# A two-layer cross-attention kernel: the order of three engines in layer 2 written out, five step places per slot, and image values masked in DRAM

## The chip, the core and the metric

The kernel runs on one core of a Trainium2 chip. TensorE (PE in the profile) multiplies matrices into PSUM; VectorE (DVE), ScalarE (ACT) and GpSimd (POOL) do the elementwise work; SyncE (SP) issues nearly all DMA transfers, and ScalarE issues a few. Each engine takes its instructions in the order in which they stand in its own stream, and waits on semaphores for what other engines and transfers deliver. The metric is the device time of one launch in microseconds, lower is better; a run is compared with runs of the kernel before on the same chip.

## The reference

Two cross-attention layers follow each other on 16 sequences of 256 tokens (width 320, 20 heads of 16). The context has 252 text tokens (77 in layer 1) and image tokens; the last 4 (layer 1: all behind the first 77) are the image tokens. Layer 2, cut to what matters:

```python
q = heads(hidden_states @ W_q)
probs_t = softmax(einsum(q, heads(text_ehs @ W_k)) * attn_scale)
text_out = einsum(probs_t, heads(text_ehs @ W_v))
attn_scores = einsum(q, heads(ip_ehs @ W_k_ip)) * attn_scale
qsem = _l2norm(einsum('bhst,bte->bhse', probs_t, text_ehs))
sem = einsum('bhse,bne->bhsn', qsem, _l2norm(ip_ehs))
probs_ip = softmax(attn_scores + SEM_SCALE * sem) * spatial_mask
out = (text_out + einsum(probs_ip, heads(ip_ehs @ W_v_ip))) @ W_out + b_out + residual
```

Layer 2 needs the norm of a probability-weighted context row for each head and token (`_l2norm` of `qsem`). The kernel gets it from the Gram matrix G of the context: the norm squared is p^T G p, with p the unnormalised probabilities.

## The kernel before

The work is cut into slots of four heads: five slots (groups) per sequence, so 80 slots in layer 1 (k = 0 to 79) and 80 in layer 2 (k = 80 to 159), with two more to drain. A slot of layer 2 (`slot1`, L866) emits, in this order:

- `both1(k, 0)` (L774): transposed scores of slot k into PSUM tile T (L788), plain scores of slot k + 2 into S (L793). VectorE takes the row maxima of S (L794) and copies the image scores out (L810); ScalarE takes the exponentials of T (L800). S has a single buffer (`scores`, L92), so the next scores wait for L794 and L810.
- `attend1(k-2)` (L855): the sum of probabilities times values (L861) and of the norms (L863) into PSUM tile P; then `settle1` (L896): VectorE transposes P (L906), divides (L909, L910).
- `both1(k, 1)`, the other half of the tokens.
- `norm1(k-1, u, n)` (L843), four calls: p^T G in PSUM (L848, four or three matmuls of 128x512), multiplied by p on VectorE (L851) and summed (L853: on GpSimd for u = 0, on VectorE for u = 1).
- `rounded1(k, u)` (L834): the high half of p on ScalarE (L838), the low half on GpSimd (L839).
- `stacks(k + 4)`: SP loads the stacked queries and keys of slot k + 4; `maxima(k + 2)`: the maxima of slot k + 2 turned (L826), copied by ScalarE (L828) and sent by two transfers that ScalarE itself issues (L830).

All else of layer 2 is done by tasks, which are Python generators cut into steps: `k1` the keys (L466), `t1` the values and G (L471), `o1` the queries (L524, L528, L529), `i1` the image softmax (L917), `c1` the closing of a sequence (L964: `finish`, L754, with the output projection L520 and the residual L767). Each step has a due time in slots relative to the sequence's first slot; `fill(now)` (L1021) runs the steps that are due. A slot before has three places for steps, at 0.33, 0.67 and 1.0.

A matrix operand is used as a high and a low half, so most PSUM results are copied by ScalarE (the high half) and then subtracted by VectorE (the low half): L148 for keys, L529 for queries, L489, L495, L499 for G, L750, L752 for the closing. The context is split by ScalarE and GpSimd (L147, L148 with the tile cta).

The image values come in `image_softmax`: four rows of `vipd` are broadcast into the tile vb (its tile is named rs in the profile, L957), VectorE multiplies them by a mask (L961), and `close1` multiplies the result by the image probabilities on TensorE (L968). vb has one buffer.

What sets the order: only TensorE's stream stands as the code emits it (L1136, `manual_schedule(engines=PINNED)`). The streams of the other engines, SP's too, are put in order by the framework's scheduler.

## Time and profile before

| | us |
|---|---|
| median of 3 runs | 1527.03 (1524.84 to 1532.59) |
| the profiled execution's own time | 1525.5 |
| its span, first to last instruction | 1523.4 |
| granted TensorE clock, mean | 0.987 |
| start of layer 2's slot 80, first L788 | 696.0 |
| start of slot 159, the last with scores | 1491.3 |

The rows of the profile name a line of the kernel, an engine, and the tiles as output<-input. In a view of windows each pair is the busy time and the number of instructions of an engine in that stretch. In the chain of waits, each row is a start, a length and a piece of work; it is followed back from the end, and jumps to whatever released a piece.

### The profile page before, as it was taken

What the parts mean: (1) busy time and instruction counts of PE and PEld (TensorE: products, weight loads), DVE (VectorE), ACT (ScalarE), POOL (GpSimd) and SP (SyncE); (2) the same over time, 40 slices, a digit from 0 to 9 for tenths busy, and PEclk for the clock granted to TensorE, in tenths of its full rate; (3) what the DMA queues carried; (4) which work ended last, traced back from release to release, by engine and by line L of the source; (5) the groups of instructions that cost most, each with busy time, mean ns of one, the idle gap of its engine ahead of it and who ended that gap; (6) DMA issues with size and microseconds to landing.
All of it is one profiled execution on the core that took longest, in us unless ns stands there. A gap on an engine that the chain in (4) does not pass through costs nothing.

```text
span 1523.4 us, 35306 instructions
## 1 busy us (share of the span) xinstructions
PE 1452.4 (95%) x12522; PEld 1196.4 (79%) x12522; DVE 1180.6 (77%) x2584; ACT 956.0 (63%) x2073; POOL 1142.2 (75%) x1161
## 2 busy tenths in 40 slices
PE   7799999999999999799999999999999999999997
PEld 6788888888888878577777877777777777777765
DVE  5467676767676777777888888888888888788896
ACT  5557676767676866656656556656665665556563
POOL 3259797979797967787778678767877787778785
PEclk9899999999999999899999999999999999999999
DMA  6666565656565665465424443443444343434311
GB/s 217 165 176 175 163 175 163 175 162 175 163 175 163 168 182 136 104 188 171 156 86 138 121 139 115 127 130 109 136 117 138 108 144 110 150 98 120 115 42 59
DMA packets 226971, 215.38 MB, mean 141 GB/s; under 512 B 49714, under 2 KB 210708, under 8 KB 226796
## 3 DMA queue, kind: packets, MB, share of 16 engines
q1 hardware_dynamic: 225056, 211.83, 48.4%
q8 instruction: 100, 1.64, 0.5%
q10 hardware_dynamic: 1740, 1.30, 0.3%
q14 instruction: 75, 0.61, 0.2%
HBM read 122.17 MB, written 89.49 MB: 139 GB/s over the span
## 4 chain that ended last, share of the span: by engine, by line
PE 72%; POOL 10%; DVE 6%; DMA 5%; issue 3%; ACT 3%; SPq 0%; ACTq 0%; POOLq 0%; DVEq 0%
PE X L212 21%; PE X L848 14%; PE X L520 10%; PE P L711 7%; POOL wt L839 6%; PE S L650 5%; PE T L673 4%; PE T L788 3%; DMA rs<-vipd 3%; PE P L861 2%; DVE mn L794 2%; PE S L793 2%; POOL wt L853 2%; PE P L863 1%; PE X L569 1%
## 5 line engine op out<-in xcount | busy, mean ns | idle before, releaser
L679 POOL TENSOR_TENSOR P<-P,rs 128x512 f32<-128x512 f32 x320 | 411.4, 1307 | 161.3 <-ACT P L676 161.1
L839 POOL TENSOR_TENSOR wt<-P,ctb 128x512 f32<-128x512 f32 x212 | 271.0, 1292 | 117.7 <-ACT ctb L838 117.7
L848 PE MATMUL X<-ctb,gm 128*128 128x512 f32 x1120 | 293.7, 402 | 0.0
L676 ACT ACTIVATE P<-T 128x512 f32<-128x512 f32 x320 | 174.8, 593 | 106.2 <-PE T L673 99.1
L848 PEld LDWEIGHTS X<-ctb,gm 128*128 128x128 f32 x1120 | 199.5, 188 | 46.4 <-issue 0.4
L794 DVE TENSOR_REDUCE mn<-S 128x4 fp32r<-128x1008 f32 x160 | 191.6, 1197 | 31.3 <-PE S L793 31.3
L851 DVE TENSOR_TENSOR wt<-X,wt 128x512 f32<-128x512 f32 x240 | 164.2, 685 | 31.1 <-PE X L848 30.1
L800 ACT ACTIVATE P<-T 128x512 f32<-128x512 f32 x212 | 114.8, 593 | 47.7 <-PE T L788 47.2
L838 ACT ACTIVATE ctb<-P 128x512 fp32r<-128x512 f32 x212 | 124.2, 625 | 32.0 <-PE X L848 30.5
L652 DVE TENSOR_REDUCE mn<-S 128x4 fp32r<-128x716 f32 x160 | 142.5, 891 | 0.0
L711 PE MATMUL P<-P,vr 128*32 128x256 f32 x1920 | 126.9, 395 | 5.3 <-DVE mx L575 2.8
L520 PE MATMUL X<-hq,wE 128*128 128x256 f32 x768 | 114.4, 292 | 4.7 <-ACT hq L509 3.5
L520 PE MATMUL X<-ho,wF 128*128 128x256 f32 x768 | 108.6, 284 | 4.8 <-DVE ho L752 4.0
L212 PE MATMUL X<-cta,wA 128*128 128x252 f32 (+1 forms) x720 | 105.4, 290 | 7.3 <-ACT wA L147 5.8
L520 PEld LDWEIGHTS X<-hq,wE 128*128 128x128 f32 x768 | 103.6, 194 | 9.1 <-ACT hq L509 4.0
L520 PEld LDWEIGHTS X<-ho,wF 128*128 128x128 f32 x768 | 102.0, 190 | 9.9 <-DVE ho L752 4.4
L839 POOL TENSOR_TENSOR wt<-qsl,ctb 128x512 f32<-128x512 f32 x54 | 69.2, 1293 | 51.9 <-ACT ctb L838 49.8
L853 POOL TENSOR_TENSOR wt<-wt 128x512 f32<-128x512 f32 x80 | 103.3, 1292 | 0.0
L212 PEld LDWEIGHTS X<-cta,wA 128*128 128x128 f32 x720 | 93.8, 194 | 11.9 <-ACT wA L147 6.1
L722 DVE STREAM_TRANSPOSE nt<-P 128x512 f32<-128x512 f32 x80 | 57.1, 713 | 51.9 <-PE P L711 51.9
L147 ACT CAST kst<-X 128x252 fp32r<-128x252 f32 (+3 forms) x94 | 35.1, 373 | 95.3 <-PE X L212 75.5
L711 PEld LDWEIGHTS P<-P,vr 128*32 128x32 f32 x1920 | 56.5, 112 | 46.6 <-issue 9.6
(217 smaller groups left out, 3383.2 us busy)
## 6 DMA issues: line engine op xcount, KB each, us to landing
qd<-q SPq DMA_DIRECT2D x96, 384.0 KB
kd<-kst SPq DMA_DIRECT2D x73, 256.0 KB
rawc<-in_cT_dram SPq DMA_DIRECT2D x60, 256.0 KB
ks<-kd SPq DMA_DIRECT2D x160, 96.0 KB
qs<-qd SPq DMA_DIRECT2D x160, 96.0 KB
qs<-qd SPq DMA_DIRECT2D x60, 192.0 KB
ks<-kd SPq DMA_DIRECT2D x60, 192.0 KB
kd<-kst SPq DMA_DIRECT2D x21, 512.0 KB
```

The lines of the kernel that those rows point to most:

```text
L212: last = mm(out, lhs(a, k), rhs(b, k), start=i == 0, stop=i == len(terms) - 1)
L520: mm(pp, w(s, k, slice(m * 128, (m + 1) * 128)), a[:, t], start=i == 0, stop=i == len(terms) - 1)
L652: anchor(nc.vector.tensor_reduce(mn[:, t, 1], sp[:, :, T0:], axis=AX.X, op=ALU.max))
L676: exp = anchor(nc.scalar.activation(pt, st[p], AF.Exp, scale=SCALE))
L679: anchor(nc.gpsimd.tensor_mul(pt, pt, rs[:, t : t + 1].to_broadcast([128, 2, S])))
L711: mm(pv[32 * s : 32 * s + 32, o : o + S], v[:, vt, h : h + 32], P[k, s // 2][:, t, s % 2], start=vt < 2, stop=vt != 1,)
L794: anchor(nc.vector.tensor_reduce(maxes[k + 2][:, t], sp[:, :, :T1], axis=AX.X, op=ALU.max))
L838: nc.scalar.activation(R[k, u][:, t], P[k, u][:, t], AF.Copy, scale=0.5)
L839: anchor(nc.gpsimd.tensor_sub(W[k, u][:, t], P[k, u][:, t], f(R[k, u][:, t])))
L848: mm(yp, gm[:, gb], R[k, u][:, kt], start=i == 0, stop=i == len(blocks[n]) - 1)
L851: nc.vector.tensor_mul(product, yp, w[:, n])
L853: (nc.vector if u else nc.gpsimd).tensor_add(w[:, 0], w[:, 0], product)
```

## The change

Instructions on the engines are the same but for one: VectorE's multiplication by the mask (16 times) is gone. TensorE has the same 10555 matmuls, in another order. Five things change.

1. In slots 80 to 159 ScalarE, VectorE and GpSimd also keep the order in which the code emits them. SP's stream is still ordered by the scheduler. Slots 0 to 79 and the end are as before.
2. The slot has five places (0.2, 0.4, 0.6, 0.8, 1.0). `attend1` and `settle1` are parted: the sums go to TensorE where they were, the transposes and divisions come behind the 0.2 place. `stacks` and `maxima` stand at the end, in the order maxima, stacks.
3. The tasks' due times are new (a table, STEPS), on multiples of 0.2.
4. `late`: VectorE's low halves, sums of residuals and other late pieces go onto a list while `hold` is in force, from just before `rounded1(k, 1)` to `release` behind the next slot's `both1(k+1, 0)` and `attend1`; so they stand behind a row maximum. `settled()` empties the list at once wherever a following step needs them. `after_next` puts a low half behind the next unit of work.
5. The masked image values are made once in DRAM: task `w8` zeroes `spread_d` [16, 128, 384] and copies `vipd` into its places; `image_softmax` loads vb from there, some steps earlier. The mask tile is gone. The transposed sums hT have two buffers, and the last sequence's residual another tile.

```diff
+    def late(*makes):
+        if held[0]:
+            lates.extend(makes)
+        else:
+            for make in makes:
+                make()
...
+    def release():
+        held[0] = False
+        settled()
+    def settled():
+        while lates:
+            lates.pop(0)()
+    def after_next(make):
+        soon.append([2, make])
...
+    def weights8():
+        zero = buf("kb", [128, 3, 2, 96], FR, bufs=2, name="zero").rearrange("p a b c -> p (a b c)")
+        nc.gpsimd.memset(f(zero), 0.0)
+        yield
+        for b in range(0, B, 4):
+            dma(spread_d[b : b + 4].rearrange("b p c -> p b c"), zero[:, :CP].unsqueeze(1).to_broadcast([128, 4, CP]))
+            yield
+        for i in range(3):
+            for half in range(2):
+                row = 4 * min(2 * i + half, NG - 1)
+                for s in range(4):
+                    lo = 128 * i + 32 * s + 16 * half
+                    src = vipd.rearrange("(b n) c -> b n c", n=NIP)[:, :, lo : lo + 16]
+                    dma(spread_d[:, 32 * s + row : 32 * s + row + NIP, lo : lo + 16], src)
+                yield
...
         def evac(m, pp):
             nc.scalar.copy(qh[:, 0, m], pp)
-            nc.vector.tensor_sub(qh[:, 1, m], pp, f(qh[:, 0, m]))
+            late(lambda: nc.vector.tensor_sub(qh[:, 1, m], pp, f(qh[:, 0, m])))
 
         yield from project(l, wq[l], a, evac)
         qd = dram.tile([3, CP, S], F32, tag=f"qd{l}", name=f"qd{l}", bufs=2)
+        settled()
...
         for s in range(4):
             mm(pv[32 * s : 32 * s + 32, :S], zone, W[k, s % 2][:, 0, s // 2], start=False, stop=True)
-        settle1(b, g, pv)
+        return b, g, pv
...
+        summed = []
         if k > NS + 1:
-            yield lambda: attend1(k - 2)
+            yield lambda: summed.append(attend1(k - 2))
+        yield release
         yield lambda: both1(k, 1)
         if last:
             yield lambda: norm1(last, 0, 0)
-        yield 0.33
+        yield 0.2
+        for parts in summed:
+            yield lambda: settle1(*parts)
         if last:
             yield lambda: norm1(last, 0, 1)
         if mine:
             yield lambda: rounded1(k, 0)
-        yield lambda: stacks(k + LEAD)
+        yield 0.4
         if last:
             yield lambda: norm1(last, 1, 0)
+        yield 0.6
+        if last:
             yield lambda: norm1(last, 1, 1)
         if mine:
+            yield hold
+        if mine:
             yield lambda: rounded1(k, 1)
-        yield 0.67
+        yield 0.8
         yield lambda: maxima(k + 2)
+        yield lambda: stacks(k + LEAD)
         yield 1.0
...
+        vb = w1["vb"]
+        if hi == NG:
+            while b and ("taken", B + b - 1) not in results:
+                step(("c1", b - 1))
+            dma(vb, spread_d[b])
...
-        vb = w1["vb"]
-        dma(vb, vipd[NIP * b : NIP * (b + 1)].unsqueeze(0).to_broadcast([32, NIP, CP]))
         yield
         pT = w1["pT"]
-        nc.vector.transpose(pT, pi.rearrange("p f c -> p (f c)"))
-        nc.vector.tensor_mul(vb, vb, w1["bmask"])
+        late(lambda: nc.vector.transpose(pT, pi.rearrange("p f c -> p (f c)")))
...
+    STEPS = {
+        "k1": (-7, -6.2, -5.8, -5, -4.6, -3,),
+        "t1": (-3.2, -2.2, -2.2, -1.4, -0.4,),
+        "o1": (-6.8, -6.8, -6, -5.8, -4, -4,),
+        "i1": (6.8, 7.6, 7.6, 8.8, 9.2, 9.6, 10.6, 10.8, 10.8, 12.2,),
+        "c1": (12.8, 12.8, 13.4, 14, 14.2, 15.8,),
...
+    with tc.manual_schedule(engines=PINNED):
+        run(range(NS))
+    with tc.manual_schedule(engines=PINNED | {getattr(mybir.EngineType, e) for e in ("Activation", "DVE", "Pool")}):
+        run(range(NS, 2 * NS))
+    with tc.manual_schedule(engines=PINNED):
+        run(range(2 * NS, 2 * NS + 2))
         fill(999)
```

In a middle sequence of the changed kernel the five slots hold, beside the scores, attention and norms: (0) keys and two projections; (1) keys and values; (2) two image products, values, one half of G; (3) one image product, the other half of G, two projections; (4) two projections and keys. Before, they held: (0) projection, keys, projection; (1) values, projection, values; (2) both halves of G; (3) two projections, image product; (4) image product, keys, image product, projection, keys.

More of the change, by code (lines that the diff above doesn't have):

```diff
@@ L114, in buf, with hold, unit @@
         return t
+    held, lates, soon = [False], [], []
+    def late(*makes):
[4 more added lines that the diff above has]
+                make()
+    def hold():
+        held[0] = True
+    def release():
[6 more added lines that the diff above has]
+        soon.append([2, make])
+    def unit():
+        for x in soon[:]:
+            x[0] -= 1
+            if not x[0]:
+                soon.remove(x)
+                x[1]()
     def const_tile(shape, tag, dtype=F32):
@@ L465, in keys1 @@
             prod(kp, lambda s, k: w1["k"](s, k, ms), lambda s, k: ct(s, k)[:, :T1], 4)
-            halves(kst[:, 0, 0, :T1], kst[:, 1, 0, :T1], kp)
             nc.gpsimd.tensor_copy(kst[:, :, 0, T1:], f(kip[:, :, m, 4 * b : 4 * b + 4]))
-            keys_out(kd[1][b], m, kst)
+            nc.scalar.copy(kst[:, 0, 0, :T1], kp)
+            late(
+                lambda kst=kst, kp=kp: nc.vector.tensor_sub(kst[:, 1, 0, :T1], kp, f(kst[:, 0, 0, :T1])),
+                lambda kst=kst, m=m: keys_out(kd[1][b], m, kst),
+            )
             yield
@@ L510, in split @@
         order(eng.tensor_sub(hl[:, 3:5], src[:, 0:2], f(hl[:, 0:2])))
-        order(nc.vector.scalar_tensor_tensor(hl[:, 2], f(hl[:, 2]), neg, src[:, 2], op0=ALU.mult, op1=ALU.add))
+        third = lambda: order(
+            nc.vector.scalar_tensor_tensor(hl[:, 2], f(hl[:, 2]), neg, src[:, 2], op0=ALU.mult, op1=ALU.add)
+        )
+        if clock[0] >= NS:
+            after_next(third)
+        else:
+            third()
         return hl
@@ L632, in stacks1 @@
         qd = get("o1", b)
+        settled()
         for u in range(2):
@@ L947, in image_softmax @@
         z4 = small(1, "z4")
-        nc.vector.tensor_reduce(z4, a, axis=AX.X, op=ALU.add)
-        nc.vector.reciprocal(z4, z4)
+        late(
+            lambda: nc.vector.tensor_reduce(z4, a, axis=AX.X, op=ALU.add),
+            lambda: nc.vector.reciprocal(z4, z4),
+        )
         yield
+        settled()
         pool.tensor_mul(z4, z4, mk.unsqueeze(1).to_broadcast([128, n, 8]))
@@ L969, in rows @@
             nc.vector.tensor_add(hp, hT[:, p], hp)
-        y = yield from finish(1, b, load(x1d[b], "xc"), rows)
-        dma(out_d[b].rearrange("(k p) t -> p k t", p=128), y)
+        y = yield from finish(1, b, load(x1d[b], "xc" if b < B - 1 else "xq"), rows)
+        late(lambda: dma(out_d[b].rearrange("(k p) t -> p k t", p=128), y))
     def close0(b):
@@ L1135, in xattn2, with run @@
         begin()
-    with tc.manual_schedule(engines=PINNED):
-        for k in range(2 * NS + 2):
+    def run(slots):
+        for k in slots:
             clock[0] = k
```

114 lines of the change are left out of this document (70 added, 44 removed), and 16 rows, old and new, of the table STEPS.

## The prediction

> **What bounds the kernel now.** I read the page first, then windows by stage, windows over the five slots of one middle sequence, and the chain of waits through it.
>
> ```profile
> span 1523.4 us, 35306 instructions
> ...
> PE 1452.4 (95%) x12522; PEld 1196.4 (79%) x12522; DVE 1180.6 (77%) x2584; ACT 956.0 (63%) x2073; POOL 1142.2 (75%) x1161
> ```
>
> TensorE is busy 95% of the span, but a waiting matmul counts as busy, so that share is no floor. By stage (start:end length, then the busy time and count of PE, PEld, DVE, ACT, POOL, the clock, the DMA share, GB/s):
>
> ```profile
> 580.00:696.00 116.00, 101.90 (x946) 82.28 (x938) 89.07 (x192) 70.72 (x148) 92.61 (x86) 0.96 0.55 151
> ...
> 845.00:1362.60 517.60, 506.17 (x4181) 402.37 (x4180) 432.98 (x900) 308.39 (x670) 391.99 (x431) 1.00 0.42 126
> ...
> 1491.30:1523.40 32.10, 22.69 (x169) 16.03 (x168) 21.31 (x53) 9.03 (x22) 16.58 (x26) 0.99 0.18 60
> ```
>
> Layer 2's steady part is ten sequences in 517.6 us, 51.76 each. The clock is full there (1.00), so nothing is to be had from it. One sequence, slot by slot:
>
> ```profile
> 1000.30:1010.70 10.40, 9.94 (x85) 7.94 (x84) 8.66 (x17) 5.07 (x11) 5.27 (x7) 1.00 0.24 79
> 1010.70:1021.70 11.00, 11.00 (x92) 8.92 (x90) 8.45 (x17) 6.20 (x14) 8.93 (x12) 1.00 0.71 216
> 1021.70:1030.90 9.20, 9.20 (x83) 7.41 (x82) 8.23 (x19) 6.19 (x13) 6.48 (x10) 1.00 0.28 61
> 1030.90:1040.30 9.40, 9.15 (x77) 6.96 (x76) 7.54 (x18) 6.59 (x15) 8.60 (x10) 1.00 0.47 134
> 1040.30:1052.10 11.80, 11.37 (x93) 9.00 (x92) 10.56 (x23) 6.83 (x16) 9.94 (x10) 1.00 0.43 127
> sum 51.80, PE 50.67 PEld 40.23 DVE 43.44 ACT 30.87 POOL 39.20; mean PE 10.13 PEld 8.04 DVE 8.69 ACT 6.17 POOL 7.84
> ```
>
> And the chain of waits through it (start, length, work):
>
> ```profile
> 1000.57 0.04 DVE rs L961
> 1000.61 1.05 issue
> 1001.66 0.41 DVE kst L148
> 1002.06 1.11 DVE mn L794
> ...
> 1003.40 0.50 PE S L793 x4
> 1003.91 1.13 PE X L848 x4
> 1005.04 0.95 PE X L520 x8
> 1005.99 1.39 PE X L212 x12
> 1007.38 2.32 PE X L848 x10
> ...
> 1010.66 0.12 PE X L826 x2
> 1010.78 0.43 PE T L788 x4
> 1011.21 0.24 PE S L793 x4
> 1011.45 1.00 PE P L861 x16
> ...
> 1014.79 1.75 PE X L212 x12
> ...
> 1023.41 0.43 PE P L863 x8
> ...
> 1025.65 1.44 PE X L212 x12
> ...
> 1042.32 2.49 POOL wt L839 x2
> 1044.81 1.26 POOL cta L148
> ...
> 1049.26 0.45 PE X L968 x2
> ```
>
> These rows give TensorE's pieces without waits. Every slot has T and S twice, sums, norms and maxima: 2 x (0.43 + 0.24) + 1.00 + 0.43 + 1.13 + 2.32 + 0.12 = 6.34 us. A projection is 0.95, keys 1.39, values 1.75, half of G 1.44; an image product 0.25 (from its 0.45, less about 0.2 of drain that the next piece overlaps, an estimate). By slot: 6.34 + 0.95 + 1.39 + 0.95 = 9.6 against 10.4; 6.34 + 1.75 + 0.95 + 1.75 = 10.8 against 11.0; 6.34 + 2 x 1.44 = 9.2 against 9.2; 6.34 + 1.9 + 0.25 = 8.5 against 9.4; 6.34 + 0.5 + 2 x 1.39 + 0.95 = 10.6 against 11.8. The third slot comes out exactly, so the method holds. Floor 48.7 us, **loss 3.0 us per sequence**, in the first and the last two slots. VectorE, 43.4 of 51.8, is the next engine, GpSimd 39.2.
>
> **The change part by part.** *The mask multiplication.* In the chain it stands at a place where TensorE waits: VectorE waited for vb to land, multiplied, and only then came to the maximum on which the single S buffer hangs. Its row, its wait, and beside them the one other large VectorE operation with both inputs in SBUF, the third piece of hq:
>
> ```profile
> L961 DVE TENSOR_TENSOR rs<-rs,nt x16: 557/932/1200, 704.9 to 1509.1; 128x384 f32<-128x384 f32 x16
> ...
>   DMA rs<-vipd: 11.8, 15
> ```
>
> ```profile
> L511 DVE SCALAR_TENSOR_TENSOR hq<-hq,tmask,xq x32: 428/477/1504, 19.1 to 1389.0; 128x256 fp32r<-128x256 f32 x32
> ```
>
> Removing it frees 0.93 us of VectorE per sequence and 11.8 / 15 = 0.8 us of standing still. The first slot's loss (0.8) should go with it. VectorE's load falls to 42.5 per sequence.
>
> The spread of L961, 557 to 1200 ns, is that of an operation held up by a neighbour. The Trainium skill, SBUF — State Buffer, section "SBUF: two separate sides", says that a VectorE operation with two SBUF inputs and a GpSimd operation that reads SBUF lock each other out for a whole instruction; the trace agrees, with 1200 and 1504 ns at the top against 557 and 428 at the bottom.
>
> *The written order.* The loss of the last two slots (0.9 + 1.2) is one of order: in the chain GpSimd does two L839 pieces (2.49) and only then the second context split (1.26), on which the keys wait. In the new streams both splits stand early in the slot whose end holds the keys, ahead of GpSimd's norm sum; L853 for u = 0 stands ahead of the L839 pieces. Both have several us in hand, so the 2.1 us are recoverable. The five slots also become even: 6.34 + 1.39 + 1.9 = 9.6; + 1.39 + 1.75 = 9.5; + 0.5 + 1.75 + 1.44 = 10.0; + 0.25 + 1.44 + 1.9 = 9.9; + 1.9 + 1.39 = 9.6: still 48.7, and 42.5 / 48.7 = 87% for VectorE, so that small waits remain.
>
> *What it adds on the path.* A written order can't step around a wait. I followed VectorE's new stream against TensorE's pieces and find three such places.
> (a) At the end of slot (0), the low half of q is flushed by `settled()` ahead of the next maximum. It waits for ScalarE's copy, which stands behind the maxima's copy and two transfers that ScalarE issues:
>
> ```profile
> L830 ACTq DMA_DIRECT2D qs<-mt x160: 632/632/866, 689.3 to 1485.1; - x160
> ```
>
> The maxima's product ends about 8.7 into the slot. Copy about 0.4, two issues 1.3, q's copy 0.4: VectorE's piece starts at 11.0 and ends at 11.4, where the maximum could start at 9.65 + 0.8 = 10.45. That is 1.0 late. Second scores follow the first by T to T, 0.43 + 0.24 + 1.00 + 0.43 = 2.1, and need the maximum (1.11 plus a copy of about 0.15), so some 0.45 is in hand: 0.5 lost.
> (b) At the end of slot (2) the next T takes a PSUM bank that the closing's low half frees: about 10.0 after norms, two image sums, ScalarE's copies; 0 to 0.4, I take 0.3.
> (c) In slot (3) the last projection takes G's bank behind three low pieces: 0.3 to 0.4, I take 0.35.
> Transfers: `stacks` now goes out some 0.6 of a slot later, and SP's stream is short of slack. The trace of before has no wait of TensorE for a stack in the steady part, so this price isn't shown: bounded by 0 and by one landing, 2.9 (row below), per sequence. I take 0.15, near the lower end: a whole slot still lies between issue and use. Sum 1.3, so 3.0 - 1.3 = **1.7 us won per sequence**, and the 14 sequences between the first and the last give 24. The first shares its slots with the end of layer 1, the last lacks keys and values; half of it each, 2.
>
> *Masks in DRAM.* The zeroes are 16 x 128 x 384 x 4 B = 3.1 MB; at the 151 GB/s of the window from 580 on that is 21 us of DMA traffic where the share is 0.55, plus 24 small scatters. It falls into the last slots of layer 1, where queries and keys also pass through DRAM. Bounds: 0, if it fits between, and 14.1 (116.00 - 101.90, TensorE's idle time of that stage, doubled); I take 1, as SP's scheduler puts the pieces between the stacks.
>
> *The end.* The chain of waits at the end:
>
> ```profile
> 1506.17 2.90 DMA rs<-vipd
> ...
> 1509.09 0.04 DVE rs L961
> 1509.13 0.44 issue
> ```
>
> vb's last load is 3.4 us of the chain there. It now starts before the exponential and division of the image softmax, which then set the pace; I take 2 of 3.4 (bounds 0 and 3.4).
>
> *Sum:* 24 + 2 + 2 - 1 = 27. The profiled execution took 1525.5, 2.1 more than its span; 1498.5. The median of the runs shown is 1527.0, 1.5 above it: **1500 us**.
>
> **The rivals.**
> *All of the loss goes:* (a) to (c) are hidden because a bank or the order is better than I followed it. 14 x 3.0 = 42, with 2 x 1.5 and the end 3.4: 48 less, 1479. For it: the slots are even to 0.5 us. Against: VectorE at 87% with fixed places. 0.12.
> *One wait for another:* VectorE's order holds nearly as much as the scheduler's did, with S late in two slots of five; (a), (b), (c) at twice my price, 2.3, plus 0.3 of transfers leave 0.4 per sequence: 14 x 0.4 + 2 = 8 less, 1519. For it: three places found by hand are seldom all. 0.14.
> *GpSimd and VectorE lock each other out* at hq's third piece, L511's 1504 against 477, 1.0 us per sequence, as its new place stands beside GpSimd's: 1.7 - 1.0, 14 x 0.7 + 3 = 13 less, 1514. Against: in the new stream GpSimd has only a small copy there. 0.05. This is the rule of the SBUF page named above.
> *Stacks or maxima land late (slower):* ScalarE's L830 now stands in a fixed place, ahead of the exponentials, and some of them wait for an SP transfer that is issued in the same slot. If SP is held by the queries' round trip through DRAM, ScalarE and then TensorE wait one landing, 2.9 us, in each sequence: 1.7 - 2.9 = -1.2, 16 times, is 19 more; the end gives 2 back and the zeroes take 1: 1545. It decides from about 2 us of delay on SP. For it: keys come nearly half a slot later and their stack is wanted a slot and a half later. Against: no row with TensorE waiting on a stack before. 0.17.
> *The change doesn't do what it says* (the scheduler's order was the same in effect): 1527. The streams differ on all engines, so only 0.02.
>
> **How the numbers follow.** Main forecast 0.50, its own range 1488 to 1512; the rivals as given. 0.5% is 7.6 us, about what a measurement of this kernel can tell from no change. Faster (below 1519.4): 0.50 + 0.12 + 0.05 + half of the 0.14 = 0.74, and some of the late-landing case, which can come out mild: 0.77. Same: the other half, 0.02, and little of the rest, 0.08. Slower 0.15. The range leaves out the worst of full recovery and most of the late-landing case: 1476 to 1530.
>
> **What would show it.** A middle sequence of 50.0 us, with slots of 9.5 to 10.2; no wait of VectorE for rs; TensorE's wait for S (now L793) gone from slot (0), but 0.5 in slot (1); no wait of TensorE for the context split; VectorE about 42.5 per sequence. Wrong if TensorE waits for ks or qs, if ScalarE stands at its transfers, if the stage from 580 to 696 grows by over 3 us, or if a sequence still takes 51.5.

## The result, and the profile after

| | us |
|---|---|
| changed kernel, median of 6 runs | 1515.72 (1513.96 to 1520.13) |
| kernel before on the same chip, median of 6 runs | 1526.36 (1522.9 to 1532.59) |
| ratio, 95% interval | 0.9934 [0.9909, 0.9958] |
| profiled execution of the changed kernel, its span | 1518.7, 1516.9 |

The change is worth 0.66%, about 10 us where 27 were forecast: faster, and inside the widest predicted range (1476 to 1530), but 15.7 us above the forecast of 1500 us and outside the main forecast's own range of 1488 to 1512. The two profiled executions are 6.8 us apart, their spans 6.5.

The page of the changed kernel, its span and the load of its engines (lines of this kernel's code are about 70 to 90 higher than before: the exponentials' T is L864, S L869, the row maximum L870, the norms' matmul L926, the maxima's transfers L907):

```profile
span 1516.9 us, 35343 instructions
...
PE 1452.9 (96%) x12522; PEld 1204.3 (79%) x12522; DVE 1178.5 (78%) x2568; ACT 951.8 (63%) x2073; POOL 1145.8 (76%) x1162
```

Every engine is as busy as before to 0.7%: what the change won or lost is waiting, not work.

The windows by stage (same columns as before): the end of layer 1; the first ten slots of layer 2; ten steady sequences (slots 95 to 144).

```profile
580.00:690.70 110.70, 98.47 (x905) 81.04 (x903) 83.48 (x183) 68.61 (x145) 89.80 (x83) 0.92 0.57 152
690.70:796.90 106.20, 97.76 (x771) 76.93 (x772) 80.03 (x158) 60.69 (x131) 73.98 (x75) 0.95 0.39 118
847.40:1353.20 505.80, 501.14 (x4184) 403.88 (x4184) 433.02 (x891) 305.76 (x670) 394.00 (x431) 1.00 0.44 129
```

Beside them the same ten slots, 80 to 89, in the kernel before:

```profile
696.00:793.30 97.30, 92.76 (x772) 73.26 (x770) 81.27 (x166) 61.80 (x135) 75.85 (x80) 1.00 0.44 134
```

The steady part went from 517.6 to 505.8 us, 1.2 per sequence. The first ten slots, with 767 matmuls for 768, went from 97.3 to 106.2, and the granted clock fell to 0.95 there. Taken from the first T matmul of each slot in both traces:

| stretch | before | after | difference | forecast |
|---|---|---|---|---|
| to slot 80 | 696.0 | 690.5 | -5.5 | +1 |
| slots 80 to 89 | 97.3 | 106.2 | +8.9 | -2.7 |
| slots 90 to 149, 12 sequences | 621.2 | 607.5 | -13.7 | -20.4 |
| slots 150 to 154 | 46.3 | 48.9 | +2.6 | -1.7 |
| slot 155 to the end | 62.6 | 63.8 | +1.2 | -3 |

So this is a gain in the middle that is given back in part at both ends.

The stretches don't hold quite the same work, since the new due times put some of TensorE's pieces on the other side of a boundary. Counted by their starts in the two traces, the stretch to slot 80 has 17 matmuls of the keys fewer, slots 80 to 89 have five of them more and slots 150 to 154 twelve more; three image products fewer stand in slots 80 to 89, one projection fewer in slots 90 to 149, and these stand behind slot 155. With the lengths of the pieces (1.39 for twelve matmuls of the keys, 0.43, 0.95), the differences on equal work are, as an estimate, -3.5, +9.6, -12.8, +1.2 and -1.0. The ten steady sequences hold the same 4180 matmuls in both.

The five slots of a middle sequence, as windows:

```profile
897.90:907.60 9.70, 9.70 (x88) 7.91 (x88) 8.43 (x18) 5.72 (x12) 9.00 (x10) 1.00 0.13 43
907.60:917.70 10.10, 9.70 (x84) 7.73 (x84) 8.65 (x19) 5.40 (x11) 7.39 (x11) 1.00 0.83 263
917.70:928.00 10.30, 10.30 (x85) 8.38 (x83) 8.91 (x18) 6.33 (x16) 7.72 (x10) 1.00 0.56 159
928.00:938.70 10.70, 10.70 (x90) 8.56 (x91) 9.14 (x21) 7.09 (x18) 7.38 (x7) 1.00 0.44 116
938.70:948.40 9.70, 9.70 (x88) 7.83 (x86) 8.17 (x17) 6.01 (x13) 8.02 (x10) 1.00 0.20 58
sum 50.50, PE 50.10 PEld 40.41 DVE 43.30 ACT 30.55 POOL 39.50; mean PE 10.02 PEld 8.08 DVE 8.66 ACT 6.11 POOL 7.90
```

Slots (0) and (4) stand at 9.7, almost at their sum of 9.6; (1), (2) and (3) are 0.3 to 0.8 above theirs. The chain of waits through the same sequence says why:

```profile
905.31 0.95 PE X L587 x8
...
906.42 0.37 ACT mt L904
...
906.81 0.63 ACTq L907
...
907.48 0.63 ACTq L907
...
908.15 0.38 ACT q L595
...
908.56 0.42 DVE q L596
908.98 1.11 DVE mn L870
...
910.32 0.50 PE S L869 x4
...
923.71 0.86 PE X L1059 x4
...
927.85 0.78 PE T L864 x4
...
936.36 2.12 PE X L587 x16
```

The first eight rows are place (a) of the prediction, link by link: maxima's copy, two issues on ScalarE, q's copy, q's low half, the maximum, S. The last three rows price what the sum had estimated: two image products are 0.86 together, 0.43 each and not 0.25; the T at the start of slot (3) is 0.78 where a free one is 0.43 (place (b)); two projections in slot (3) are 2.12 instead of 1.91 (place (c)).

The start, slots 80 and 81: windows of the changed kernel, and the chain through the first of them.

```profile
698.70:704.00 5.30, 1.75 (x16) 1.17 (x14) 2.49 (x7) 3.72 (x9) 4.30 (x6) 0.88 0.49 161
704.00:710.50 6.50, 6.50 (x23) 5.08 (x21) 4.24 (x8) 2.29 (x5) 1.93 (x2) 0.58 0.60 197
```

```profile
700.41 0.64 ACTq L907
...
701.09 0.38 ACT ho L827
...
701.50 0.42 DVE ho L818
701.92 0.33 DVE q L596
...
703.61 0.80 PE S L869 x4
704.41 5.79 PE X L926 x14
```

TensorE has 1.75 us of work in 5.3 us, waiting for S behind the same kind of row: ScalarE's issues, the copy of the first layer's closing (ho), its low half, q's low half, the maximum. Then its granted clock is 0.58, and 14 norm matmuls take 5.79 us. Slot 81 is 16.0 us; before it was 11.0.

### The profile page after: what moved, and what is told of

It is laid out like the page before. It is cut to its first block, busy times and chain, and to the rows that moved or that the text cites. A ratio compares the mean times of both kernels' runs of the same rounds, so it can differ in the third digit from the quotient of the medians.

```text
span 1516.9 us, 35343 instructions
## 1 busy us (share of the span) xinstructions
PE 1452.9 (96%) x12522; PEld 1204.3 (79%) x12522; DVE 1178.5 (78%) x2568; ACT 951.8 (63%) x2073; POOL 1145.8 (76%) x1162
## 4 chain that ended last, share of the span: by engine, by line
PE 82%; DVE 6%; DMA 4%; ACT 2%; issue 2%; ACTq 1%; POOL 1%; SPq 1%; DVEq 0%; POOLq 0%
PE X L245 22%; PE X L926 17%; PE X L587 11%; PE P L780 6%; PE S L719 5%; PE T L742 4%; PE P L939 4%; PE T L864 4%; PE S L869 2%; PE P L941 2%; DVE mn L870 2%; ACTq L907 1%; PE X L637 1%; PE X L1059 1%; DMA kd<-kst 1%
## 5 line engine op out<-in xcount | busy, mean ns | idle before, releaser
L926 PE MATMUL X<-ctb,gm 128*128 128x512 f32 x1120 | 296.3, 407 | 0.7 <-ACT P L876 0.4
L870 DVE TENSOR_REDUCE mn<-S 128x4 fp32r<-128x1008 f32 x160 | 192.8, 1205 | 68.6 <-PE S L869 66.5
L926 PEld LDWEIGHTS X<-ctb,gm 128*128 128x128 f32 x1120 | 202.7, 190 | 51.2 <-ACT P L876 0.9
L929 DVE TENSOR_TENSOR wt<-X,wt 128x512 f32<-128x512 f32 x240 | 159.4, 682 | 5.5 <-PE X L926 5.5
L780 PE MATMUL P<-P,vr 128*32 128x256 f32 x1920 | 123.8, 388 | 3.6 <-DVE mx L643 2.6
L587 PEld LDWEIGHTS X<-hq,wE 128*128 128x128 f32 x768 | 101.2, 195 | 10.6 <-ACT hq L570 3.8
L245 PE MATMUL X<-cta,wA 128*128 128x252 f32 (+1 forms) x720 | 99.7, 285 | 5.5 <-ACT wA L180 5.5
L720 DVE TENSOR_REDUCE mn<-S 128x4 fp32r<-128x308 f32 x160 | 74.6, 466 | 22.8 <-PE S L719 22.7
L719 PE MATMUL S<-ks,qs 125*128 125x256 f32 x480 | 87.8, 306 | 1.2 <-DVE mn L721 1.2
```

The costliest lines, as they stand in the source:

```text
L245: last = mm(out, lhs(a, k), rhs(b, k), start=i == 0, stop=i == len(terms) - 1)
L587: mm(pp, w(s, k, slice(m * 128, (m + 1) * 128)), a[:, t], start=i == 0, stop=i == len(terms) - 1)
L719: mm(sp[:, h], Q[: XROW + T0, h, t * 128 : (t + 1) * 128], K[: XROW + T0, h], start=True, stop=True)
L780: mm(pv[32 * s : 32 * s + 32, o : o + S], v[:, vt, h : h + 32], P[k, s // 2][:, t, s % 2], start=vt < 2, stop=vt != 1,)
L870: anchor(nc.vector.tensor_reduce(maxes[k + 2][:, t], sp[:, :, :T1], axis=AX.X, op=ALU.max))
L926: mm(yp, gm[:, gb], R[k, u][:, kt], start=i == 0, stop=i == len(blocks[n]) - 1)
```

## The experiments

All kernels, with the ratio to the kernel before on the same chip, and lengths in us from the first T matmul of the slots in each profiled execution:

| kernel | median | ratio, 95% interval | slots 80-89 | slots 95-144 | slots 150-154 |
|---|---|---|---|---|---|
| before | 1526.36 | 1 | 97.3 | 517.6 | 46.3 |
| changed | 1515.72 | 0.9934 [0.9909, 0.9958] | 106.2 | 505.8 | 48.9 |
| e1 masks alone | 1517.99 | 0.9954 [0.9935, 0.9973] | 99.2 | 513.8 | 46.0 |
| e2 scheduler's order | 1519.83 | 0.9965 [0.9944, 0.9985] | 99.9 | 515.7 | 46.4 |
| e3 written from 90 | 1513.51 | 0.9927 [0.9900, 0.9954] | 95.9 | 506.7 | 48.1 |
| e4 written 90 to 149 | 1511.07 | 0.9911 [0.9884, 0.9938] | 97.6 | 505.5 | 50.6 |
| e5 q behind | 1508.80 | 0.9904 [0.9867, 0.9942] | 103.3 | 501.0 | 48.2 |
| e6 ho one unit later | 1518.43 | 0.9953 [0.9934, 0.9971] | 106.2 | 505.5 | 48.7 |
| e8 nothing held | 1545.79 | 1.0128 [1.0098, 1.0158] | 109.6 | 523.6 | 49.0 |
| e9 e5 + ho late | 1509.81 | 0.9887 [0.9853, 0.9920] | 105.7 | 501.2 | 47.4 |
| e10 mask back | 1527.94 | 1.0017 [0.9995, 1.0038] | 106.6 | 509.2 | 48.6 |
| e11 e5 + maxima by SyncE | 1527.64 | 1.0009 [0.9987, 1.0030] | 99.5 | 525.7 | 49.7 |
| e12 e5 + weights early | 1507.62 | 0.9873 [0.9838, 0.9908] | 105.4 | 501.5 | 47.5 |
| e13 e5 + SyncE at the start | 1504.82 | 0.9860 [0.9828, 0.9892] | 99.8 | 499.7 | 48.6 |
| e14 e5 + si after | 1503.07 | 0.9846 [0.9818, 0.9873] | 103.3 | 498.1 | 47.5 |
| e15 e13 + e14 | 1499.80 | 0.9823 [0.9795, 0.9852] | 100.5 | 497.7 | 47.5 |

The stretches of before and e1 differ from those of the others by the pieces named above. In e3 and e4, 21 matmuls of slot 89 stand behind the first T of slot 90, and slot 80 has five fewer, so their slots 80 to 89 hold 741 matmuls where the changed kernel's hold 767; in e4, 24 of slot 149 stand behind the first T of slot 150.

### Parting the change: masks, order, where the order begins

e1 is the kernel before with part 5 alone (the masked image values in DRAM and the task that makes them).

> The kernel before with part 5 alone: the image values masked once in DRAM, no multiplication on VectorE; places and orders as before. My sum gave the multiplication and its wait 0.8 us per sequence (slot (0) from 10.4 to about 9.6) and 2 at the end, less 1 for the zeroes: 12 less than before, about 1514, so as much as the whole change gave. The rival: VectorE's next piece takes the place of the wait, slot (0) stays over 10.1, and the time is 1522 to 1527.

The multiplication is gone, and the middle sequence falls from 51.8 to 51.4, all of it in slot (0) (10.4 to 10.0). That is half of the 0.8 that the prediction gave to it: the maximum is late for a second reason as well. In e1's trace the low half of the keys stands ahead of it and waits 1.38 us for ScalarE's copy, which stands behind the two issues of the maxima's transfers, the row of place (a).

e2 is the changed kernel with TensorE's stream alone fixed, so that the scheduler orders ScalarE, VectorE and GpSimd in layer 2:

```diff
-    with tc.manual_schedule(engines=PINNED | {getattr(mybir.EngineType, e) for e in ("Activation", "DVE", "Pool")}):
+    with tc.manual_schedule(engines=PINNED):
         run(range(NS, 2 * NS))
```

> The changed kernel with the scheduler's order on ScalarE, VectorE and GpSimd in layer 2 too; places, late pieces and masks as changed. If the written order is worth something as a whole, this is slower than the changed kernel's 1516, up to 1530. If it wins about 1.1 us per middle sequence and gives it back at both ends, the two are within 4 us, slots 80 to 86 are some 8 us shorter than in the changed kernel, and the middle sequences 0.5 to 1 us longer than 50.5.

The written order is worth 9.9 us in the ten sequences (515.7 against 505.8). Slot (3) wins 1.6 per sequence: 10.5 to 11.2 us written, 11.9 to 13.2 by the scheduler. In slot (1) the scheduler is better by 0.7, 9.46 against 10.13 and more, and at the start by 6.3 us. Slot (2) is 10.33 in both, and in all later kernels: no order decides it.

e3 and e4 begin the written order at slot 90, and e4 ends it at slot 149.

```diff
-        run(range(NS))
+        run(range(NS + 10))
...
-        run(range(NS, 2 * NS))
+        run(range(NS + 10, 2 * NS))
```

> The changed kernel with the scheduler's order up to slot 89 and the written one from slot 90 on. If the written order costs the start of layer 2 (slot 81 with 16.0 us, slots 85 and 86 with 12.2 each), this gives 6 to 9 us back: 1507 to 1510. If the start suffers from the step places or from the 3.1 MB of zeroes, it stays at 1514 to 1517.

> As the one before, and the scheduler's order again from slot 150 on. If the written order costs the end too (slots 153 and 157 with 11.3 and 9.9 us), another 2 to 4 us less: 1504 to 1507. If the end is set by its chain of waits whatever the order, the same as with the written order to the end.

Slots 81 to 88, which hold the same 624 matmuls in each of these kernels, take 82.9 and 84.6 us, against 89.0 in the changed kernel and 82.5 in e2, so the loss at the start belongs to the written order there. (The 95.9 and 97.6 of the table flatter the two, since they hold less work.) The change from one order to the other costs 2.4 us in slots 89 and 90 together (20.3 for 17.9) and 0.4 in slots 149 and 150 (19.8 for 19.4). Both medians miss their forecasts, by 3.5 and 4.1 us.

### What holds the middle: q's low half

e5 undoes one line of the change: q's low half and its transfers stay behind the maximum.

```diff
         qd = dram.tile([3, CP, S], F32, tag=f"qd{l}", name=f"qd{l}", bufs=2)
-        settled()
...
-            dma(qd[r].rearrange("(m p) t -> p m t", p=128), qh[:, s])
+            late(lambda r=r, s=s: dma(qd[r].rearrange("(m p) t -> p m t", p=128), qh[:, s]))
```

> The changed kernel, with one thing undone: the low half of q and the three transfers of q's stack stay behind the maximum on VectorE, instead of being settled ahead of it. Theory: slot (1) of a middle sequence is 10.13 us long in the changed kernel and 9.46 us with the scheduler's order, because VectorE's low half of q waits for ScalarE (copies behind two issues of 632 ns of the maxima's transfers) and the maximum, the exponentials' bias and S's next product wait behind it. With the low half behind, slot (1) goes to about 9.5 us, 0.6 less per sequence, and the time by 14 sequences to 1507 (1505 to 1510). Rival A: the maximum itself is held by ScalarE's order (the exponentials of the unit before), and slot (1) stays at 10.1, the time at 1515. Rival B: q's stack comes late for the next slot's S, slot (2) grows by 0.3 to 1.0, and the time is 1515 to 1525.

Slot (1) is 9.46 to 9.55 in each sequence from slot 90 on. The theory is shown, and place (a) is worth 0.67 per sequence. The median is 0.3% of the kernel before better than the changed kernel's (0.9904 against 0.9934; the intervals overlap), the profiled execution 11.9 us of span. Slot (2) didn't grow (rival B).

e8 takes the opposite step: nothing is held back, each low half stands ahead of the maximum again.

```diff
     def hold():
-        held[0] = True
+        held[0] = False
```

> The changed kernel with nothing held back: every piece of VectorE that the change puts behind a maximum is issued at its own place, ahead of it; the order on the engines is still written out. Theory (the third and fourth part of the change): with 3 to 5 low halves of 250 to 600 ns ahead of a maximum in slots (0), (3) and (4), each of these slots is 0.3 to 1.0 us longer, 1 to 2.5 us per sequence, and the time is 1528 to 1550. Rival: the low halves that are freed earlier (banks of T and G, stacks) give as much back, and the time is within 5 us of 1515.

It costs 1.9% (1.0128 against 0.9934), 30 us: in a middle sequence slot (0) goes from 9.66 to 10.4 and slot (4) from 9.7 to 10.65, 1.7 together. TensorE's waits for S behind VectorE's copy of the image scores, first the changed kernel, then e8:

```profile
PE S L869 <- DVE sr L886: 10.2, 19, 1.4
```

```profile
PE S L869 <- DVE sr L886: 30.2, 46, 2.3
```

So of the pieces that these runs part, the holding back of part 4 is worth the most. The changed kernel without it is slower than the kernel before.

### The mask, from the other side

e10 is the changed kernel with part 5 undone.

```diff
-        late(lambda: nc.vector.transpose(pT, pi.rearrange("p f c -> p (f c)")))
+        late(
+            lambda: nc.vector.transpose(pT, pi.rearrange("p f c -> p (f c)")),
+            lambda: nc.vector.tensor_mul(vb, vb, w1["bmask"]),
+        )
```

> The changed kernel with its fifth part undone: the image values are read without their masks from DRAM and VectorE multiplies them by the mask in slot (0), one multiplication of two tiles in SBUF per sequence. The prediction put this at 0.8 us per sequence, 11 or 12 us in all (1527). By the run that had this part alone (0.36 us per sequence in slot (0), 7 us in all) it is 1520 to 1523. Rival: with the order written out the multiplication stands behind the maximum and is hidden; the time is within 2 us of 1515.

It takes back the whole gain: 1.0017 against 0.9934, 12.7 us (8.7 in the spans of the two profiled executions). In a fixed order the multiplication isn't hidden. Three transposes of hT, the transpose of the image probabilities, the multiplication and the keys' low half all stand ahead of the first maximum of slot (2), which takes 10.8 us instead of 10.33. From the chain of e10:

```profile
915.30 1.00 DVE hT L811 x3
...
917.98 1.03 DVE rs L1055
919.01 0.33 DVE kst L519
919.34 1.11 DVE mn L870
...
920.68 0.51 PE S L869 x4
```

Another 5.9 us are behind slot 155 (69.7 us to the end, against 63.8). Of these 3.3 lie from slot 158 on, where the chain holds the load of vb again, 2.82 us, which the changed kernel's doesn't. The other 2.5 are slot 157, 12.4 us for 9.9, where the granted clock fell to 0.75; e9, e11 and e15, which have no multiplication, take 11.4 to 11.5 there, so this part isn't shown to be the mask's. The rival, a hidden multiplication, falls.

### The start of layer 2

e6 and e9 put the low half of the first layer's closing behind a unit, or onto the list of late pieces.

```diff
-            if l:
+            if l or clock[0] >= NS:
                 after_next(lambda p=p, hp=hp: low_half(hl, p, hp))
```

> The changed kernel, with the low halves of the first layer's closing (ho) that fall into slots of layer 2 put behind the next unit, as the second layer's closing has them. Theory: slots 80 to 84 take 54.2 us in the changed kernel and 47.5 to 48.0 with the scheduler's order, because in slot 81 ScalarE's ho copy, VectorE's low half of ho, q's low half and the maximum stand in a row and TensorE has nearly nothing for 5.3 us (698.7 to 704), after which its granted clock falls to 0.58 for 6.5 us. With the low halves behind, slot 81 goes from 16.0 to 11 to 12 us, slots 80 to 84 to 49 to 50, the clock stays at 1.0 there, and the time is 4 to 6 us less: 1510 to 1512. Rival: the maxima's transfers and the context's copies on ScalarE hold slot 81 by themselves; it stays at 15 to 16 us and the time at 1515.

```diff
             else:
-                low_half(hl, p, hp)
+                late(lambda p=p, hp=hp: low_half(hl, p, hp))
```

> The changed kernel with q's low half behind the maximum, and also the low half of the first layer's last closing held back until the second step of a slot of layer 2 is issued (an edit that put it one unit later left it ahead of the maximum in VectorE's order, so it did not test this). Theory: in slot 81 VectorE's maximum stands behind this low half, which waits for ScalarE's copy, which waits behind two issues of 640 ns of the maxima's transfers; with it behind the maximum slot 81 falls from 15.9 to 12 to 13 us, the nearly idle stretch of TensorE of 5 us is down to 2 to 3 us, and the granted clock of 0.58 in the 6 us after it comes back to 1.0. The time is 3 to 4 us under that of the kernel with q's low half behind alone. Rival: slot 81 stays at 15 to 16 us, since the maximum of the second half is held by the maxima's transfers themselves (the first product of S needs them).

e6 left VectorE's order around slot 81 as it was (15.9 us) and says nothing. e9 moves the piece, and slot 81 comes down by 1.4 us only, to 14.5; the hole stays, since ScalarE's exponentials stand behind the same two issues. Slot 85 grew by 1.7, so the first ten slots are no shorter than in e5.

e12 moves the steps that split the second closing's weights (`"w4": (4.2, 4.4, 5.2, 5.4,)` for `(4.6, 5, 5.4, 5.6,)`).

> The changed kernel with q's low half behind the maximum, and also the steps that split the second closing's weights moved from places late in slots 84 and 85 (0.6 and 1.0 of a slot) to early ones (0.2 and 0.4). Theory: slots 85 and 86 take 10.7 and 12.1 us because two low halves of 128x384 with both inputs in SBUF, 0.98 and 1.15 us each beside GpSimd, stand ahead of the maxima on VectorE and ScalarE's copies for them behind the transfers of the maxima; moved, slots 84 to 86 (31.6 us) go to 29 to 30 us. Rival: the slots stay as long, since in them VectorE and ScalarE have no room wherever the pieces stand.

Slots 84 to 86 took 34.2 us instead of 31.7: the theory falls, the pieces cost more at the early places.

e11 takes the two issues off ScalarE, in all of layer 2, e13 in the first nine slots only.

```diff
-                lambda u=u: nc.scalar.dma_start(
+                lambda u=u: (nc.sync if NS <= k <= NS + 8 else nc.scalar).dma_start(
```

> The changed kernel with q's low half behind the maximum, and also the transfers of the maxima of layer 2 issued by SyncE's queue instead of ScalarE's. Theory: in slot (3) of a middle sequence (10.6 us in the changed kernel, up to 12.3 in single sequences) the exponentials stand on ScalarE behind these two transfers, which wait for the stacks of keys to land; issued elsewhere, they hold nothing, and slot (3) goes to 9.4 to 10 us, 0.6 to 1.2 less per sequence and no single long ones; the time is 8 to 14 us less. Rival: on SyncE's queue they stand behind the other transfers, the products that read them come later, and the slots get 0.3 to 1 us longer each; the time is 1515 to 1540.

> The changed kernel with q's low half behind the maximum (1508.8 us in its own run), and the maxima's transfers of slots 80 to 88 issued by SyncE instead of ScalarE. Theory: at the start of layer 2 ScalarE's two issues of 640 ns, ahead of the first layer's last copies, hold VectorE's pieces and the maximum; slots 80 to 89 go from 103.3 to 99.5 us, as in the kernel that had all of these transfers on SyncE, slot (3) of the later sequences stays at 10.6 to 12.3, and the time is 3 to 4 us less, 1504 to 1506. Rival: the gain at the start belonged to other transfers that this shifted, and slots 80 to 89 stay at 102 to 104 us.

In e11 both sides were half right. The start is 3.8 us shorter than in e5, so ScalarE's issues are a good part of what held it. In the middle, the forecast of its theory failed: slot (3) grows to 12.0 to 14.9 us, 2.5 per sequence. TensorE now waits for stacks of keys, a row that the changed kernel doesn't have; it is 8.9 us in all, and what makes up the rest of the 25 wasn't parted:

```profile
PE S L868 <- DMA ks<-kd: 8.9, 15, 1.3
```

e13 keeps the gain (99.8) without the loss (499.7). It is level with the scheduler's order on the same matmuls (99.9 in e2), slot for slot it isn't: slot 81 takes 13.0 us for 10.4, slot 85 9.2 for 12.6. That wasn't parted further.

### Slot (3): who waits for whose transfer

In e5 slot (3) varies from 10.6 to 12.3. The chain of e5 through the longest one, slot 133:

```profile
1216.11 2.51 DMA kd<-kst
...
1220.64 2.56 DMA ks<-kd
...
1223.28 0.63 ACTq L906
...
1224.63 1.09 ACT P L875 x2
...
1225.77 0.97 PE X L925 x3
```

The maxima's transfers (L906 here) read nothing of the keys, and yet they start when a load of keys has landed. The compiled streams show why. Each transfer of SyncE and ScalarE raises one of eight counters, taken in turn, and a transfer is issued only when the one before it on its counter has landed. In slot (3):

```
SyncE    transfers 757 to 764   ks<-kd   counters 7 0 1 2 3 4 5 6
SyncE    transfers 765 to 768   si<-sid  counters 7 0 1 2
ScalarE  two transfers          qs<-mt   counters 3 4: wait for 761 and 762
```

e14 moves the four loads of the image scores (si) behind the pair, so that it gets counters 7 and 0 and waits for 757 and 758, the first of the eight loads instead of the fifth and sixth.

```diff
-        si = results["si", b] = buf("si", [128, 8, NG * NIP], bufs=2)
+        si = results["si", b] = buf("si", [128, 8, NG * NIP], bufs=1)
...
-            later(1.3, lambda s=s: dma(si[32 * s : 32 * s + 32], parts[:, s]))
+            later(2.6, lambda s=s: dma(si[32 * s : 32 * s + 32], parts[:, s]))
```

> The changed kernel with q's low half behind the maximum, and one buffer in place of two for the image scores that come back from DRAM, so that these four loads go out after the maxima's transfers of slot (3) and not before. In the row of transfers that SyncE and ScalarE share, each waits for the one eight places before it: the maxima's pair of slot (3) then waits for the first two of the eight key loads instead of the fifth and sixth. Theory: the wait of ScalarE's exponentials for the maxima's transfers (19.2 us in 11 waits with the pair of buffers) falls by about 1.4 us a time, slot (3) goes to 10.3 to 10.6 us with no single ones over 11, 0.4 less per sequence on the mean, 5 to 6 us in all: 1503. Rival: slot (3) is bound by its PSUM banks and the long ones by something else: it stays at 10.6 to 12.3 and the time at 1508. Second rival: the image scores come late for the image softmax and slots (3) or (4) grow by 0.5 or more.

The waits of ScalarE's exponentials into P for these transfers, first e5, then e14 (us in total, times, longest):

```profile
ACT P L875 <- DMA qs<-mt: 19.2, 11, 3.1
```

```profile
ACT P L875 <- DMA qs<-mt: 4.7, 3, 1.7
```

Slot (3) is 10.53 to 10.63 in every sequence, and the ten sequences are a standing row of TensorE work. Their window in e14 (length, then TensorE's busy time, the same):

```profile
841.00:1339.10 498.10, 498.10 (x4183) 403.00 (x4182) 432.32 (x891) 305.30 (x670) 394.06 (x431) 1.00 0.44 131
```

The theory is shown, the second rival didn't come, and the first is right in what remains: 10.6 is the slot's own length, with the banks of (b) and (c) in it. The forecast of 1503 was met; the ratio is 0.6% below e5's (on another chip), the ten sequences are 2.9 us shorter.

e15 has e13's and e14's edits together.

> The changed kernel with q's low half behind the maximum and both edits: the first nine slots' maxima by SyncE, and the image scores' loads after the maxima's transfers. Theory: the two add, 3 to 4 and 5 to 6 us, 1499 to 1501. Rival: the gain at the start changes the order of transfers for the rest too, and the time is 1504 to 1509.

They add: 1499.80 us, 1.8% under the kernel before and 16 us under the changed one, so it beats both.

## Why the prediction came out as it did

**The steady sequences: waits right, floor wrong.** The forecast was 1.7 per sequence, 3.0 of loss less 1.3 of new waits; measured, 1.2 (11.8 in the ten steady sequences, where 17 was forecast). The new waits are as priced, in sum nearly to the tenth: (a) 0.67 for 0.5 (e5), (b) 0.35 for 0.3 (the T of 0.78 for 0.43, in the same place in e14), (c) 0.21 for 0.35, and landing transfers some 0.1 for 0.15 (slot (3) at a mean of 10.7 in the changed kernel, 10.6 in e14): 1.3. (In (a) the prediction's terms, 8.7 + 0.4 + 1.3 + 0.4, give 10.8 and not its 11.0; in the trace VectorE's piece starts 10.9 into the slot.) (a) is shown by an experiment; (b) and (c) are read from the chain alone, and no run took them away. What failed is a term of the floor: the image product at 0.25, "from its 0.45, less about 0.2 of drain that the next piece overlaps, an estimate". The next piece overlaps nothing: one product is 0.43 in the chain of the changed kernel. The third slot, which came out exactly before, holds no image product and couldn't show this. Three products per sequence put the floor at 49.25 and the loss before at 2.5, not 3.0. That is 0.54 per sequence, 5.4 us in the ten, where 5.2 were missed. It also explains slot (2): 6.34 + 0.86 + 1.75 + 1.44 = 10.4, against a 10.3 that no order changed.

**The start and the end: the step that failed.** "The 14 sequences between the first and the last give 24. The first shares its slots with the end of layer 1, the last lacks keys and values; half of it each, 2." Slots 80 to 89 were thus counted at 2.7 us won; they lost 8.9, the largest of the misses. The middle's pieces aren't what those slots hold: the first layer's last closing and the second closing's weights stand in the same fixed order there, with the same row of ScalarE's issues ahead of them. The scheduler's order takes 99.9 on the same matmuls (e2), so 6.3 of the loss is the written order's: q's low half is 2.9 of it (e5), the issues 3.5 (e13 against e5). The other 2.6, 99.9 against 97.3, came with the other parts of the change: e1, with part 5 alone, takes 99.2, but e10, without part 5, is no shorter than the changed kernel (106.6), so what costs it stays open. The step had the right mechanism at hand, (a), and applied it to the middle alone. Slots 150 to 154 were counted as a middle sequence too, but the kernel before had less to lose there: without keys its slots (3) and (4) took 7.7 and 8.1. Of the 2.6 that the change lost, 1.4 is the keys' piece that had stood ahead of slot 150, and most of the rest lies in slot 153, which took 11.3 where e14 has 10.5.

**The mask.** 0.8 per sequence was the price, 11 in all. Alone (e1) the part gives 7 us, taken back from the changed kernel (e10) 12.7. The totals are near what was said, but not as the sum had it: 0.4 per sequence in the middle, half of the price. In e1's trace 7.7 of the 11.7 us of span come from layer 1, which has no such multiplication, and slots 80 to 89 take 1.9 more. That part of the agreement is luck. The prediction's 2 for the end (bounds 0 and 3.4) is borne out by e10's 3.3 us from slot 158 on; slot 155 to the end grew by 1.2 all the same, since 2.2 us of TensorE's work came in there.

**The zeroes** were put at 1 us lost, and layer 1 ended 5.5 us earlier. About 2.0 us of that is the keys' work that now stands behind slot 80. In the kernel before slot 72 took 11.4 us, in the changed one 7.1; but all other kernels here also reach slot 80 at 688 to 692, e10 without the masks in DRAM among them, and e1 with the old places too (688.3). The scheduler orders layer 1 anew for each program. So this gain needs neither part 5 nor the new places; which difference it hangs on stays open. Of the 6.5 us that the profiled execution's span fell, 5.5 (3.5 on equal work) are this gain, which nobody forecast: that the time came out clearly below the kernel before is in part luck.

**The rivals.** The time lies nearest to two of them, one wait for another (1519) and the lock between GpSimd and VectorE (1514). The first didn't happen: the three places cost in sum what was forecast. Of the second, VectorE grew by the 1.0 us per sequence that was named, mostly on another operation (last section); but that time isn't on the chain of the middle, where the floor and the three places leave nothing for it. Late stacks and maxima, the slow rival at 2.9 per sequence, came in mild form, and its mechanism was seen only in part: ScalarE's issues do wait for stacks in flight, but through the counter that they share and not because of their data. Of its signs, ScalarE standing at its transfers came: the exponentials into P stood there for 14.6 us in 8 waits in the changed kernel, and not once before. Sent over SyncE (e11) the case is nearly as forecast: 2.5 per sequence and no gain left. Of what was to show the steps right, VectorE's wait for rs is gone, no row waits for the context split, but VectorE's load stayed at 43.3 per sequence instead of 42.5.

## What to carry to other kernels

Here the written order won where every slot is alike and lost where one stage runs into the next; work out the stage's first and last rounds by themselves before multiplying a middle round by their number. In a fixed order, ask of each piece ahead of a maximum (or any other release of a single buffer) what it waits for: a low half behind a copy behind two transfer issues cost 0.67 us in each sequence, and holding such pieces back is what made the change pay at all. Where transfers take completion counters in turn, a small urgent one waits for a large one some places before it; moving unrelated loads behind it cost nothing here and was worth 0.3 us per sequence.

## What the runs showed of the hardware

The granted TensorE clock fell after one thin stretch, and the price came afterwards. In the changed kernel 1.75 us of work in 5.3 us was followed by a clock of 0.58 over 6.5 us, in which 14 norm matmuls took 5.79 us instead of the 3.42 that they take in the middle. e13 had 2.78 us of work in 4.8 us and fell as well; e2 had 3.90 in 5.0 us at about the same place and didn't. From windows of e13, then of e2:

```profile
696.20:701.00 4.80, 2.78 (x21) 2.04 (x21) 3.60 (x11) 3.86 (x11) 4.80 (x6) 1.00 0.18 59
701.00:705.00 4.00, 3.86 (x12) 3.04 (x13) 2.30 (x4) 1.27 (x3) 1.39 (x3) 0.57 0.84 282
```

```profile
697.00:702.00 5.00, 3.90 (x28) 3.02 (x27) 4.78 (x11) 3.36 (x9) 2.77 (x4) 1.00 0.74 244
702.00:707.30 5.30, 5.30 (x40) 4.99 (x39) 3.22 (x6) 2.81 (x7) 5.16 (x5) 1.00 0.39 127
```

The Trainium skill, TensorE: Matmul & The Clock Gate, section "Part 1: The HAM clock gate", has the clock halve after an idle window of about 3.4 us and return after a busy one. A clock of 0.57 and 0.58 in windows that hold the return agrees with a halved one (a window from 703 to 709 of the changed kernel shows 0.50); but the stretches here weren't idle, TensorE was busy for 33% and 58% of them. A hole of 5 us on such a chain therefore costs more than its own length: here some 2.4 us more (5.79 less 3.42).

TensorE's busy share alone doesn't decide it. At the start of slot 157 it was busy for 4.68 of 6.0 us in e15, and the clock fell; in the changed kernel it was busy for 4.69 of 6.0 us at about the same place, and the clock stayed at 1.00, in the 3.6 us behind it too. What decides isn't shown. From windows of e15, then of the changed kernel:

```profile
1449.00:1455.00 6.00, 4.68 (x48) 2.58 (x46) 5.93 (x13) 3.12 (x8) 5.33 (x7) 1.00 0.08 26
1455.00:1458.60 3.60, 3.60 (x11) 2.83 (x10) 3.12 (x8) 1.87 (x5) 2.64 (x5) 0.53 0.10 25
```

```profile
1467.00:1473.00 6.00, 4.69 (x46) 2.67 (x46) 5.90 (x14) 3.13 (x7) 5.33 (x8) 1.00 0.13 44
```

VectorE lost one operation of 0.93 us per sequence and was as busy as before (432.98 us in ten sequences before, 433.02 after). Two others have grown by as much. From the groups of VectorE's work in the steady stretch, the kernel before (busy time, mean ns of one):

```profile
L511 DVE SCALAR_TENSOR_TENSOR hq<-hq,tmask,xq 128x256 fp32r<-128x256 f32 x10 | 4.8, 477 | 0.0
...
L927 DVE SCALAR_TENSOR_TENSOR u<-u,tmp 128x40 f32<-128x40 f32 x10 | 1.9, 195 | 0.0
```

The changed kernel, and from its timeline one of these operations beside GpSimd's:

```profile
L1011 DVE SCALAR_TENSOR_TENSOR u<-u,tmp 128x40 f32<-128x40 f32 x10 | 9.4, 937 | 0.0
...
L573 DVE SCALAR_TENSOR_TENSOR hq<-hq,tmask,xq 128x256 fp32r<-128x256 f32 x10 | 7.4, 740 | 0.0
```

```profile
923.82 1.28 POOL L931 TENSOR_TENSOR wt<-wt 128x512 f32<-128x512 f32 x1 [0.96 <-DVE wt L929]
```

```profile
924.26 0.94 DVE L1011 SCALAR_TENSOR_TENSOR u<-u,tmp 128x40 f32<-128x40 f32 x1
```

The same 128x40 operation takes 937 ns instead of 195, the third piece of hq 740 instead of 477: 1.0 us per sequence together. In the written order each of them stands at a fixed place, and here L1011 starts inside GpSimd's sum (923.82 to 925.10) and ends 0.1 us behind it. By the Trainium skill, SBUF — State Buffer, section "SBUF: two separate sides", a VectorE operation with two SBUF inputs and a GpSimd operation that reads SBUF lock each other out for a whole instruction, and the trace agrees with its 937 ns. No run here moved the two apart, so the cause is read from the times and not shown by an experiment.
